# Masked attention with residual: the row step and the norm of a pair each one step later in the hand-written order

## The chip, the cores and the metric

The kernel runs on one core of one Trainium2 chip. The metric is the device time of one execution in microseconds (us), lower being better. A core has the engines TensorE (PE, matmuls; its weight loads are listed as PEld), VectorE (DVE), ScalarE (ACT), GpSimd (POOL), which here mainly issues gathers and scatters, and SyncE (SP), which here issues all other transfers. SBUF is the on-chip memory, PSUM the small memory that TensorE writes to.

## The reference

Sixteen batches of a tensor `x` (512 channels by 1024 tokens) go through an attention with eight heads of 64 channels. A token whose mask is 0 takes no part as a key, and as a query it gets equal scores, which is the mean over all tokens. The result is added to `x`.

```python
xt = transpose(x)                            # (16, 1024, 512)
q  = xt @ Wq.T                               # queries, keys and values are the same
scores = 0.125 * einsum('bhqd,bhkd->bhqk', qh, qh)
logits = (scores * cmask + (1 - cmask) * -1e30) * rmask
ctx = einsum('bhqk,bhkd->bhqd', softmax(logits), qh)
out = x + transpose(ctx @ Wo.T)
```

About half of the tokens are unmasked. What the kernel does exploits that.

## The kernel before, in words

For each batch `b` the unmasked tokens, at most 544 of them, are gathered into a compact list. Only these go through scores, softmax and the projection; their result is added to their rows of `x` and scattered back. The masked tokens all get the same vector (the projection of the mean), added elsewhere. Products are made from float16 parts, high and low (`xh` and `xl`, `ch` and `cl`, `wqh` and `wql`), so one product is three matmuls.

The eight heads are worked as four pairs `p` = 0 to 3. A batch is a list `S` of 18 steps: four steps (p, i), i = 0 to 3, for each pair, each for 128 of the keys, and two steps (0, None) at place 2 and (1, None) at place 13 for the last 32 keys of four heads together. In the list, pair 0 ends at step 4, pair 1 at step 8, pair 2 at step 12 and pair 3 at step 17.

What a step issues, in this order:
- jobs that were put in the dictionary `free` for this step;
- the scores of the first head of the pair (L620, four matmuls into `pss`, of which there are two buffers; then the exponential on ACT, L624, which also sums the rows into `z`);
- a share of the batch's other work, the list `m`, given out by `fill` in proportion to fixed costs: queries of the next batch (L447 with its ACT copy L450, the split into `hl` L461 to L463 on DVE, and the copies `xx` L468 to L471 on SP), values (L497, L500), value tails (L520, L523), transposes of the gathered rows (L424, with L384 on ACT and L385 on DVE), the mean token's columns (L381, L382), the shift of the softmax (L541, L543, L549, L551, L558, L560 and the lines to L572), and projections of the batch before (L727 on PE, L732 on DVE);
- the scores of the second head, and at i = 1 the attends of the pair before (L643, 16 matmuls into `pav`) at a raised priority;
- at i = 2 the last part of the pair before (L647, four matmuls, which need the copies `pt` that L604 and L605 prepare on DVE and L611 and L612 issue on SP), and the copy of `pav` to `c` on ACT (L651).

A pair's softmax sums become a factor for each query in three jobs:
- `recip_sums` (L666 to L674, DVE): from the sums in `z` and `zt` the reciprocals, a column `rcol` for the pair; two such columns are used in turn.
- `recip_rows`: PE transposes the column (L680) into a `pm` buffer, DVE copies ten rows out (L683, `rr`, raised priority), SP writes them to DRAM (L685, `rd`) and reads them back twice as rows broadcast over 64 partitions each (two issues of L688, `rb`, two buffers).
- `norm` (DVE): L711 multiplies `c` by `rb`, L712 adds the mean's part, L714 and L715 split into `ch` and `cl`, L716 and L717 do the same for the last 32 queries; for pair 0 also L707 and L708. L711 is held behind the latest scores or query matmul at the moment of its issue (`self.beat`), except for pair 3.

For pairs 0 to 2 these jobs are put into `free` when the pair's last step `st` is issued: the sums for `st + 2`, the rows for `st + 3`, the norm for `st + 7`, at most the last step, 17. The norm of pair 2 is put there only in the last batch; in the others it stands in the list `m` of the next batch (named `second` there). Pair 3's three jobs all stand in the next batch's `m` (`sums`, `rows`, `third`).

So in a batch the rows of pairs 0, 1 and 2 are issued at steps 7, 11 and 15, and the norms of pairs 0 and 1 at steps 11 and 15.

Issue order is not yet the order on the engines. A list scheduler with priorities orders the instructions of each engine, the raised ones ahead; buffers are taken from pools (`pm`, `pss` two each, `rb` two, `c` four, `p` twelve), and an engine works its instructions strictly in its order. A waiting instruction holds up all behind it on its engine.

Of the kernel before, what the change touches and what calls it, by code (L numbers as in the profile page):

```python
# [49 lines left out]
class Fast:  # L50
# [794 lines left out]
    def run(self, flag):  # L845
        B = self.B
        L = lambda f, *a: lambda: f(*a)
# [3 lines left out]
        N = len(S)  # L851
# [93 lines left out]
        if True:  # L945
            for b in range(B + 1):
# [4 lines left out]
                free, sums, rows, third, tail, rest = {}, [], [], [], [], []  # L951
# [68 lines left out]
                def fill(part, end=False):  # L1020
                    nonlocal done, goal, pos
                    goal += part * unit
                    while pos < len(m) and (end or (part and done + m[pos][0] / 2 <= goal)):
                        m[pos][1]()
                        done += m[pos][0]
                        pos += 1

                for st, (p, i) in enumerate(S):
                    soon, self.soon = self.soon, []
                    for f in soon + free.get(st, []):  # L1030
                        f()
                    if i is None:
                        self.scores(b, p, None)
                    else:
                        ps = [self.scores(b, 2 * p, i)]
                        if i == 2 and whole:
                            whole.pop()()
                    fill(share[st][0], st == N - 1)
                    if i is not None:
                        ps.append(self.scores(b, 2 * p + 1, i))  # L1040

                    for _ in range(1 if b < B - 2 else -(-len(self.urgent + self.spare) // (N - st))):
                        self.issue()

                    if i == 0:
                        ready, todo = todo, []
                    elif i == 1:
                        self.group_first = None
                        for f in ready[3::-1] + ready[4:]:
                            f()  # L1050
                        ready = []
                    fill(share[st][1])
                    if i is not None:
                        todo.append(L(self.attend, b, p, i, ps))
                    if i == 3:
                        (whole if p < 3 else todo).append(L(self.attend, b, p, 4, None))
                        if p < 3:
                            free.setdefault(st + 2, []).append(L(self.recip_sums, b, p))
                            free.setdefault(st + 3, []).append(L(self.recip_rows, b, p))
                            if p < 2 or b == B - 1:  # L1060
                                free.setdefault(min(st + 7, N - 1), []).append(L(self.norm, b, p))
                self.st.pop(b - 4, None)
        bad = self.const.tile([1, 1], F32, name="bad")
        self.nc.vector.tensor_reduce(bad, self.ok[0:1, :], AX.X, ALU.add)
# [145 lines left out]
```

## Time and profile before

| | |
|---|---|
| three timed runs | 1070.66, 1070.85 and 1076.17 us, median 1070.85 |
| the profiled execution | 1064.91 us, its span 1063.1 us |
| granted TensorE clock in it | 0.992 |
| DMA | 181.37 MB moved, mean 171 GB/s |
| one batch | about 63.3 us |
| L711 on DVE, 64 times | 722 ns each |
| L624 (exponential) on ACT, 512 times | 718 ns each |
| L620 on PE, 2048 matmuls | 307.0 us busy, 6.5 us idle before them |
| L680 on PE, 64 times | PE idle before them: 6.3 us until `rcol` L674 (9 times), 0.7 us until the exponential L624 (once) |

The page was taken from one execution by the hardware profiler. "Busy" is the time that an engine's instructions took; the ends of matmuls are modelled, and they overlap. A line such as `PE pm L680 <- DVE rcol L674` says that PE sat idle ahead of the instruction at line 680 that writes the tile `pm`, until the instruction at line 674, which writes `rcol` on DVE, was done. A timeline row has the start in us, the duration in us, engine, line, operation, out and in tiles with their sizes, how many like it in a row, and in brackets the idle time ahead of it and what ended it.

### The profile page before, as it was taken

How to read it: one execution, taken by the hardware profiler on the slowest of the kernel's cores; microseconds unless marked ns; L12 is line 12 of the kernel's file. 1: busy time of each engine (PE TensorE's matmuls, PEld its weight loads, DVE VectorE, ACT ScalarE, POOL GpSimd, SP SyncE). 2: the span in 40 equal slices, each digit the busy share in tenths (PEclk: the TensorE clock that was granted, in tenths of full speed). 3: DMA queues.
4: the chain of work that ended last, by engine and by line, in shares of the span. 5: the costliest groups of instructions: out<-in, count | busy, mean ns of one | idle time of the engine just before them, and what ended most of it. 6: DMA issues, size and time to landing. Idle time of an engine off the chain costs nothing.

```text
span 1063.1 us, 23765 instructions
## 1 busy us (share of the span) xinstructions
PE 1021.6 (96%) x8626; PEld 701.6 (66%) x8626; DVE 729.2 (69%) x2376; ACT 672.5 (63%) x1722; POOL 298.6 (28%) x303
## 2 busy tenths in 40 slices
PE   7798999999999999999999999999999999999996
PEld 7576666666666767666676666767666676766553
DVE  6697668676766856776775766876676776666653
ACT  5876666666676766666676576676666676664550
POOL 3101013322301222332322223232232332235652
PEclk9899999999999999999999999999999999999998
DMA  6746555546654665766557575655856554575752
GB/s 206 226 132 166 136 166 165 177 142 204 174 145 137 160 189 156 195 194 165 173 149 210 167 199 172 162 166 148 239 174 179 170 159 144 142 195 170 222 172 76
DMA packets 78123, 181.37 MB, mean 171 GB/s; under 512 B 15008, under 2 KB 16800, under 8 KB 78000
## 3 DMA queue, kind: packets, MB, share of 16 engines
q1 hardware_dynamic: 56816, 111.62, 38.4%
q0 software_dynamic: 21184, 68.18, 20.5%
q8 instruction: 70, 1.15, 0.5%
q14 instruction: 53, 0.43, 0.1%
HBM read 92.34 MB, written 33.91 MB: 119 GB/s over the span
## 4 chain that ended last, share of the span: by engine, by line
PE 76%; ACT 10%; DVE 7%; issue 3%; DMA 2%; POOL 0%; POOLq 0%; DVEq 0%; SPq 0%; ACTq 0%
PE pav L643 22%; PE pss L620 17%; PE pm L727 15%; PE pm L447 12%; ACT p L624 5%; PE pm L424 2%; PE pav L647 2%; ACT xh L384 1%; DVE p L605 1%; ACT xm L369 1%; PE pss L595 1%; PE pm L497 1%; PE pm L680 1%; ACT v L500 1%; ACT p L599 1%
## 5 line engine op out<-in xcount | busy, mean ns | idle before, releaser
L624 ACT ACTIVATE p<-pss,nm 128x544 f32<-128x544 f32 x512 | 365.4, 718 | 217.5 <-PE pss L620 203.6
L620 PE MATMUL pss<-xx 128*128 128x272 f16 x2048 | 307.0, 280 | 6.5 <-ACT p L624 5.7
L643 PE MATMUL pav<-p,v 128*64 128x272 f32 x2048 | 248.8, 396 | 0.0
L620 PEld LDWEIGHTS <-xx 128*128 128x128 f16 x2048 | 194.7, 99 | 63.3 <-issue 22.5
L643 PEld LDWEIGHTS pav<-p,v 128*64 128x64 f32 x2048 | 141.4, 137 | 91.0 <-issue 13.9
L811 POOL DMA_INDIRECT y_out<-xa,idx x68 | 72.1, 1060 | 292.8 <-PE pss L620 150.2
L447 PE MATMUL pm<-xh,wqh 128*128 128x274 f16 (+1 forms) x512 | 143.9, 281 | 2.4 <-DVE xa L732 1.9
L447 PE MATMUL pm<-xh,wql 128*128 128x274 f16 (+1 forms) x512 | 143.2, 280 | 0.0
L447 PE MATMUL pm<-xl,wqh 128*128 128x274 f16 (+1 forms) x512 | 143.1, 280 | 0.0
L339 POOL DMA_INDIRECT xa<-x_in,idx x68 | 67.9, 999 | 210.6 <-PE pss L620 101.5
L447 PEld LDWEIGHTS <-wqh 128*128 128x128 f16 x1024 | 98.1, 99 | 25.8 <-issue 4.8
L624 ACT ACTIVATION_READ_ACCUMULATOR p<-pss,nm 128x1 f32 x512 | 104.0, 203 | 0.0
L811 POOL DMA_INDIRECT y_out<-xi,idx x60 | 69.5, 1159 | 107.5 <-PE pss L620 49.0
L727 PE MATMUL pm<-woh,ch 128*128 128x512 f16 x240 | 91.1, 380 | 0.0
L727 PE MATMUL pm<-woh,cl 128*128 128x512 f16 x240 | 90.9, 379 | 0.0
L727 PE MATMUL pm<-wol,ch 128*128 128x512 f16 x240 | 90.9, 379 | 0.0
L450 ACT ACTIVATE q<-pm 128x272 f32<-128x272 f32 (+1 forms) x128 | 50.9, 398 | 63.0 <-PE pm L447 62.8
L339 POOL DMA_INDIRECT xi<-x_in,idx x60 | 61.4, 1023 | 102.2 <-PE pss L620 43.5
L732 DVE SCALAR_TENSOR_TENSOR xa<-pm,xa 128x512 f32<-128x512 f32 x60 | 41.3, 688 | 63.3 <-PE pm L727 59.9
L727 PEld LDWEIGHTS <-ch 128*128 128x128 f16 x480 | 45.6, 98 | 45.9 <-issue 1.4
L798 DVE TENSOR_TENSOR xi<-xi,ub 128x512 f32<-128x512 f32 (+1 forms) x60 | 40.9, 688 | 42.6 <-PE pss L620 42.0
L711 DVE TENSOR_TENSOR c<-c,rb 128x544 f32<-128x544 f32 x64 | 46.2, 722 | 28.0 <-PE pm L447 17.1
(194 smaller groups left out, 1558.4 us busy)
## 6 DMA issues: line engine op xcount, KB each, us to landing
xx<-hl SPq DMA_DIRECT2D x256, 136.0 KB
xm<-x_nat_in SPq DMA_DIRECT2D x56, 512.0 KB
rb<-rd SPq DMA_DIRECT2D x128, 136.0 KB
pt<-c SPq DMA_DIRECT2D x64, 136.0 KB
pt<-p SPq DMA_DIRECT2D x64, 136.0 KB
ub<-ud SPq DMA_DIRECT2D x16, 256.0 KB
xi<-x_nat_in SPq DMA_DIRECT2D x8, 256.0 KB
xa<-x_in,idx POOLq DMA_INDIRECT x68, 4.6
```

What stands on the lines that cost most here:

```text
L339: dma = self.nc.gpsimd.indirect_dma_start(out=tile[:n], out_offset=None, in_=self.x, in_offset=bass.IndirectOffsetOnAxis(ap=idx, axis=0))
L424: self.pe = nc.tensor.transpose(pt[:, c, :], x[:n, c * P:(c + 1) * P], self.ident[:n, :n]).ins
L447: self.beat = nc.tensor.matmul(pq, lhsT=w[:, c, e * P:(e + 1) * P], rhs=xx[:, c, cols], start=(k == 0), stop=(k == 3 * DC - 1)).ins
L450: nc.scalar.activation(s["q"][:, e, cols], pq, AF.Copy, scale=1.0 / (SX * SW))
L620: self.beat = nc.tensor.matmul(pt[:, g, :CH], lhsT=xx[:, 2 * k, i * P:(i + 1) * P], rhs=xx[:, 2 * k + a, g * CH:(g + 1) * CH], start=(a == ...
L624: self.exp = [nc.scalar.activation(t.rearrange("p (g c) -> p g c", g=2), pt[:, :, :CH], AF.Exp, bias=s["nm"][p // HG][:, p % HG:p % HG + 1 ...
L643: mm = nc.tensor.matmul(s["pav"][k * DK:(k + 1) * DK, g, :CH], lhsT=s["v"][p][:, i, k * DK:(k + 1) * DK], rhs=ps[k][:, cols], start=(i == ...
L711: self.once(nc.vector.tensor_tensor(c, c, s["rb"][p], ALU.mult), self.beat if p < 3 else None)
L727: nc.tensor.matmul(po[:cols.stop - cols.start], lhsT=a[:, e, cols], rhs=w[:, e, :], start=(e == 0 and k == 0), stop=(e == DC - 1 and k == 2))
L732: self.nc.vector.scalar_tensor_tensor(x, po, 1.0 / (SX * SW), x, ALU.mult, ALU.add)
L798: self.once(self.nc.vector.tensor_tensor(x[:n], x[:n], s["ub"][:n], ALU.add), self.beat)
L811: dma = self.nc.gpsimd.indirect_dma_start(out=self.out, out_offset=bass.IndirectOffsetOnAxis(ap=idx, axis=0), in_=x, in_offset=None)
```

## The change

Two numbers in `run` change. The rows of pairs 0, 1 and 2 are put into `free` for four steps after the pair's end, not three: steps 8, 12 and 16. The norms of pairs 0 and 1 are put there for eight steps after it, not seven: steps 12 and 16. In the last batch the norm of pair 2 stays at step 17, the last one, while its rows move. The sums (`recip_sums`) stay where they are, as do pair 2's norm in the other batches and all of pair 3. No instruction is added or removed on any engine; their order changes.

```diff
                         if p < 3:
                             free.setdefault(st + 2, []).append(L(self.recip_sums, b, p))
-                            free.setdefault(st + 3, []).append(L(self.recip_rows, b, p))
+                            free.setdefault(st + 4, []).append(L(self.recip_rows, b, p))
                             if p < 2 or b == B - 1:
-                                free.setdefault(min(st + 7, N - 1), []).append(L(self.norm, b, p))
+                                free.setdefault(min(st + 8, N - 1), []).append(L(self.norm, b, p))
```

## The prediction

> **What bounds the kernel now.** I read the share of busy time first, then the chain that ended last, then what TensorE (PE) waited for. The first line below is busy time per engine, the second the chain's share per engine.
>
> ```profile
> PE 1021.6 (96%) x8626; PEld 701.6 (66%) x8626; DVE 729.2 (69%) x2376; ACT 672.5 (63%) x1722; POOL 298.6 (28%) x303
> PE 76%; ACT 10%; DVE 7%; issue 3%; DMA 2%; POOL 0%; POOLq 0%; DVEq 0%; SPq 0%; ACTq 0%
> ```
>
> PE is the bound nearly everywhere, and the change adds no instruction to any engine, so only PE's idle gaps can move. Going through PE's records one by one I count 73 gaps of together 29 us, about 12 of them in the first 100 us. That is what there is to win or to double. The view of waits names those gaps (wait: us in total, times, longest):
>
> ```profile
> PE pm L680 <- DVE rcol L674: 6.3, 9, 0.7
> PE pss L620 <- ACT p L624: 5.7, 13, 0.7
> PE pm L447 <- DVE xa L732: 1.9, 5, 0.4
> PE pm L680 <- ACT p L624: 0.7, 1, 0.7
> ```
>
> The dearest repeated gap is the very instruction that is moved, the transpose L680 of `recip_rows`: ten times, always pair 2 (batches 1, 3, 4, 6, 7, 9, 10, 12, 13, 14), 0.70 us each (batch 14: 0.63). Batch 6 shows how (PE, DVE and SP rows in order of time):
>
> ```profile
> 463.98 0.28 PE L558 MATMUL pm<-ident,m 128*128 128x4 f32 x2
> 464.65 0.17 DVE L674 TENSOR_TENSOR rcol<-rcol,hit 128x10 f32<-128x10 f32 x1
> 464.76 0.73 DVE L711 TENSOR_TENSOR c<-c,rb 128x544 f32<-128x544 f32 x1
> 464.97 0.30 PE L680 MATMUL pm<-ident,rcol 128*128 128x128 f32 x1 [0.70 <-DVE rcol L674]
> 467.64 0.19 DVE L717 TENSOR_TENSOR ctl<-c,cth 128x32 f16<-128x32 f32 x1
> 471.56 0.17 DVE L381 CAST xh<-ms 128x4 f16<-128x4 f32 x1 [3.72 <-PE pm L447]
> 476.28 0.69 DVE L732 SCALAR_TENSOR_TENSOR xa<-pm,xa 128x512 f32<-128x512 f32 x1 [1.02 <-PE pm L727]
> 476.89 0.41 DVE L523 TENSOR_TENSOR tmp<-pm,par 128x256 f32<-128x256 f32 x1
> 477.23 1.04 PE L424 MATMUL pm<-ident,xa 128*128 128x128 f32 x8
> ```
>
> PE reaches L680 before DVE has made `rcol`; then pair 1's norm (L711 to L717) follows, and DVE idles 3.72 us before L381. From L381 to L732 it works with 1.02 us of idle time, and L424, which needs the buffer that L732 empties, starts 0.26 us after L732's end. Those two lines are the cover that the change uses up.
>
> **The change part by part.** The two programs' instruction orders, set side by side without running, show where the steps go. Each L680 keeps its 0.11 us of PE (start to the next start).
>
> *Pair 2's rows, step 15 to 16.* L680 now stands behind a dozen of L447 (1.4 us) and more, so `rcol` is ready: −0.70 in each of batches 1, 3, 4, 6, 7, 9, 10, 12, 13.
>
> *Pair 1's norm, step 15 to 16.* In those nine batches L711 to L717 and L683 now stand between L381 and L732. I add start-to-start times: L711 0.64, L712 0.30, L714 0.33, L715 0.60, L716 and L717 0.20, L683 0.20, less L708 (0.17, now behind L523). Interleaved with L382 to L485 they close some 0.4 us of small waits for results that the old order has, so DVE reaches L732 5.35 us after L381 instead of 4.72, while PE's product is there at 4.83 (one L680 more in between). L732 is 0.52 late, L424 has 0.26 of cover, so a new stall of about 0.3. Without the closing it is 0.8; if DVE packs tighter, 0. I take 0.3, because the old rows already start 0.07 to 0.08 us before the one ahead ends where nothing depends.
>
> Batches 3, 6, 7, 9, 10, 12, 13: −0.70 + 0.30, seven times: **−2.8**. In batches 1 and 4 the bottom's first matmul L549 also comes after only half a group of scores and waits for L543, which stands behind pair 0's norm and an L732: about 0.5 more, bounds 0 and 1.0. Two times +0.1: **+0.2**.
>
> *Batches 2, 5, 8, 11.* Here L447's wait for L732 (0.37 to 0.45) goes: −1.6. The norm of pair 0 and an L732 now stand ahead of L604 and L605, so the two `pt` copies are issued 1.7 us later and land 0.7 to 1.0 later; the attend L647 that needs them also comes 0.86 earlier on PE in some of these batches. Their landings have a margin of 0.45 us in batch 2, 1.60 in 5, 1.83 in 8 and 0.63 in 11. So two batches pay 0.2 to 0.4: **−1.0** (bounds −3.5 with the earlier L647 kept as gain, +2.5 with a late copy in all four).
>
> *Batch 14* has both stalls (0.45 and 0.63) and the last batches' dense gathers: **−0.5**, bounds −1.1 and +0.5. *Batch 0*: three groups of scores now follow each other without other work between, and PE stalls of L620 for the exponential are 0.4 to 0.7 long: **+0.75**, bounds 0 and 1.5.
>
> *Pair 0's rows, step 7 to 8.* In seven batches L680 now stands five score groups' matmuls ahead of L520, and that needs the buffer that L683 empties: about 0.1 each, **+0.7**, bounds 0 and 2. Pair 1's rows meet no wait either way. In the last batch pair 2's rows move and its norm stays at step 17; there L711 already waits 1.53 us for `rb`, but the projections that need it have about 1.4 us of margin: 0, bounds 0 and +2.
>
> *SP's queue and pair 2's norm in the next batch.* This norm does not move, its data do. Of each moved step the DMAs L685 (`rd`) and two L688 (`rb`) move too. Before:
>
> ```profile
> DVE c L711 <- DMA rb<-rd: 4.4, 5, 1.5
> SPq L688 <- DMA rd<-rr: 83.5, 45, 4.6
> 471.25 1.11 SPq L688 DMA_DIRECT2D rb<-rd  x2
> 473.61 0.48 SPq L468 DMA_DIRECT2D xx<-hl  x1
> ```
>
> L685 now passes the 512 KB load L374 and the `pt` copies (its landing was 5.05 us behind them, 1.2 alone), but L468 now stands between `rd` and `rb` and waits for L463, which comes 2.2 us later behind pair 1's norm. By batch 6's clock: rows at 472.7, L468 at 475.8, L688 at 476.3 and 476.85. An `rb` lands 2.3 to 4.8 us after its issue in the DMA records, so at 479.2 to 481.6. DVE comes to L711 at about 478.7, and behind L711 stand both L385, which free the buffers for the next L424 at about 482.9. L711 and the two L385 take 1.95, so DVE may wait 2.2 to 2.6 us before PE notices. The wait is 0.5 to 2.9; I take its middle, which is hidden: **0**, bounds 0 and +0.7 for each of 13 batches.
>
> [...]
>
> **The sum.** −2.8 + 0.2 − 1.0 − 0.5 + 0.75 + 0.7 + 0 = −2.65 us. The profiled execution took 1064.91 (span 1063.1): it becomes 1062.3. The three timed runs have their median at 1070.85, 0.55% above that execution, so I put the same difference on the median: **1068.2**. A measurement of this kernel can tell about 0.5% (5.35 us) from no change, and this forecast lies inside: no difference that counts, with a lean to faster.
>
> **Rivals.**
> *Full gain.* If DVE packs tighter than I add, no new stall follows at L424, L549 and L647: ten stalls (6.9) and five (2.1) go, and batch 0 and pair 0's rows give back 1.45: −7.6, so 1063.3. For it speaks DVE's 69% and the 3.72 us hole just ahead; against it, that the hole lies before L381 and the norm now behind it. Chance 0.31, with the cases between this and the forecast beyond −5.35.
> *DVE blocked by a late `rb`.* Place: L711 of pair 2's norm at the head of DVE's queue in the next batch, with both L385 behind it. Price: 0.5 to 1.0 us of PE in 13 batches, +6.5 to +13 on the sum, so 1074.7 to 1081.2. It decides at a landing later than about 4.5 us after the issue of L688 (a DVE wait over 2.4 us), since the nearest rows end at 4.8 and L374 and four `xx` copies of 136 KB are issued around it. Against it: most landings lie under 3.5. With the case that the norm behind L381 costs its full 0.8 us in nine batches (+4.5 on the sum) and more at L549: chance 0.27.
> *The change does nothing.* The wait is only handed from L680 to L424 one for one, and the rest cancels: 1070 to 1072. This belongs to the forecast's side of the bounds.
>
> **Chances and range.** Within 0.5%: 0.42 (forecast, and the change that does nothing). Faster 0.31. Slower 0.27. Likeliest case alone: 1065.5 to 1073. The range that should hold 8 in 10 goes from the full gain with batches 2 to 11 at their good end (1061.5) into the blocked DVE at a little under half its price (1077.0).
>
> **What would show it.** Right: the wait of L680 for L674 vanishes from PE's list; a new wait of L424 for L732 of about 0.3 us appears some nine times; L447's wait for L732 shrinks; DVE's idle time before L381 grows to about 6 us and that before L732 vanishes; DVE's wait of L711 for `rb` grows from 4.4 to 10 us or more, while L424's wait for L385 stays away. Wrong: L424 waits for L385 over ten times (the blocked DVE), L647 waits for `pt` in most batches, or L680 still waits. If PE's gaps sum to within 3 us of 29 and the time still moves by over 0.5%, the whole way of counting gaps is wrong.

## The result, and the profile after

The changed kernel is slower: 1087.42 us (median of 4, 1085.91 to 1091.26) against 1071.03 us of the kernel before in the same runs. The ratio is 1.0154, with a 95% interval of 1.0135 to 1.0173. The forecast was 1068.2, its range ended at 1077.0. The profiled execution after took 1088.17 us, its span is 1086.5 us. The two spans differ by 23.4 us, more than the medians, because the first trace of the kernel before lies 6 us below its timed runs.

The two lines of the page that answer to those shown before (busy time, and the chain that ended last):

```profile
PE 1031.7 (95%) x8626; PEld 702.4 (65%) x8626; DVE 720.3 (66%) x2376; ACT 672.0 (62%) x1722; POOL 366.2 (34%) x303
PE 73%; ACT 7%; DMA 7%; DVE 6%; issue 4%; POOL 1%; SPq 1%; POOLq 0%; another core or an unknown queue 0%; DVEq 0%; ACTq 0%
```

The same number of matmuls has 10 us more of busy time, and DMA has gone from 2% of the chain to 7%. The view of PE's waits (us in total, times, longest) says where:

```profile
PE pav L647 <- DMA pt<-p: 10.9, 5, 3.2
PE pss L620 <- ACT p L624: 9.4, 13, 2.9
PE pm L424 <- DVE xa L732: 0.4, 1, 0.4
```

L680 is gone from the list, as forecast, and so is L447's wait for L732. In their place stands L647, the last part of pair 2's attend, waiting for the copies `pt`. Counted over all PE records, the idle gaps rise from 29.4 to 42.7 us.

To see which batches pay, I cut each batch in two at its two groups of tail scores (L595, at steps 2 and 13) and compare the pieces with the kernel before. A second trace of that kernel (e0, below) repeats 27 of the 29 pieces from batch 1 on within 0.02 us (the other two differ by 0.18 and 1.31), so differences of 0.1 us count. The four columns are the pieces from step 13 of batches 2, 5, 8 and 11 to step 2 of the next (26.5 us each before); the last is the mean of the same piece of batches 3, 6, 7, 9, 10, 12 and 13. All in us against the kernel before; the experiments are described below.

| kernel | 2 | 5 | 8 | 11 | mean of seven |
|---|---|---|---|---|---|
| changed | +3.53 | +4.18 | +2.05 | +4.57 | −0.24 |
| e3, pair 0 alone | +1.13 | +1.30 | +0.98 | +3.49 | −0.53 |
| e4, pair 1 alone | +1.20 | −0.51 | −0.51 | +0.78 | +0.32 |
| e5, pair 2's rows alone | +0.03 | +0.03 | +0.04 | +0.03 | −0.65 |
| e8, pairs 0 and 1 | +2.48 | +3.92 | +3.49 | +4.21 | −0.44 |
| e9, pairs 1 and 2 | +0.34 | −0.56 | −0.57 | −0.57 | −0.49 |
| e6, changed, no wait for `pt` | −0.52 | −0.51 | −0.51 | −0.52 | −0.09 |
| e7, changed, warm matmuls | +1.79 | +1.76 | +1.65 | +1.82 | −0.40 |
| e12, changed, norm 0 back in four | +1.26 | −0.58 | −0.57 | −0.37 | +0.07 |
| e14, changed, load later in four | +2.57 | +0.57 | +1.15 | +3.90 | −0.19 |

Four batches lose 14.3 us together; nearly all of the rest lies at the two ends of the run (see "The ends" below). Batch 5 of the changed kernel shows how the loss is made. First DVE and SP of the changed kernel in order of time:

```profile
400.20 0.69 DVE L798 TENSOR_TENSOR xi<-xi,ub 128x512 f32<-128x512 f32 x1 [5.05 <-PE pss L620]
403.17 0.70 DVE L711 TENSOR_TENSOR c<-c,rb 128x544 f32<-128x544 f32 x1
405.71 0.67 DVE L715 TENSOR_TENSOR cl<-c,ch 128x512 f16<-128x512 f32 x1
407.20 0.48 SPq L468 DMA_DIRECT2D xx<-hl  x1
407.65 0.28 DVE L463 COPY hl<-hl 128x544 f16<-128x544 f16 x1
407.94 0.42 DVE L604 CAST c<-p 128x544 fp32r<-128x544 f32 x1
408.44 0.71 DVE L605 TENSOR_TENSOR p<-p,c 128x544 fp32r<-128x544 f32 x1
409.13 1.04 SPq L471 DMA_DIRECT2D xx<-hl  x1
410.27 0.55 SPq L611 DMA_DIRECT2D pt<-c  x1
411.16 0.81 SPq L612 DMA_DIRECT2D pt<-p  x1
```

The same steps in the kernel before (the whole is 7.7 us earlier there; its L595 group starts at 395.46, the other at 403.15):

```profile
387.49 0.72 DVE L711 TENSOR_TENSOR c<-c,rb 128x544 f32<-128x544 f32 x1
392.69 0.69 DVE L798 TENSOR_TENSOR xi<-xi,ub 128x512 f32<-128x512 f32 x1 [2.36 <-PE pss L620]
397.85 0.29 DVE L463 COPY hl<-hl 128x544 f16<-128x544 f16 x1
398.14 0.44 DVE L604 CAST c<-p 128x544 fp32r<-128x544 f32 x1
400.50 0.54 SPq L611 DMA_DIRECT2D pt<-c  x1
401.15 0.76 SPq L612 DMA_DIRECT2D pt<-p  x1
```

Before, pair 0's norm ran at 387.49, ahead of a hole of 2.36 us in DVE's work. Now it stands at 403.17, behind that hole, which has grown to 5.05 us, and inside the split of the third query block. Counted from the start of the L595 group, L604 starts at 4.79 us instead of 2.68, and the first `pt<-p` is issued at 8.02 instead of 5.69, behind four `xx` copies which wait for the same split. It lands at 13.6 instead of 10.1 (landings from the DMA's semaphore records). PE wants L647 at 10.95, before at 11.71. So it waits, and then something else happens (PE's rows):

```profile
416.89 0.62 PE L647 MATMUL pav<-pt,vt 128*128 128x272 f32 x3 [2.79 <-DMA pt<-p]
417.95 0.29 PE L447 MATMUL pm<-xh,wqh 128*128 128x274 f16 x1
418.08 0.28 PE L447 MATMUL pm<-xl,wqh 128*128 128x274 f16 x1
419.02 0.43 PE L447 MATMUL pm<-xh,wqh 128*128 128x274 f16 x1
419.24 0.43 PE L447 MATMUL pm<-xl,wqh 128*128 128x274 f16 x1
```

The window of that stretch (us, then busy time and instructions of PE, PEld, DVE, ACT and POOL, granted clock, DMA share, GB/s):

```profile
418.00:421.00 3.00, 3.00 (x16) 2.07 (x16) 0.60 (x6) 1.79 (x5) 0.00 (x0) 0.55 0.26 95
```

The matmuls behind the wait first follow each other in 0.12 us, then in 0.23, and the granted clock is 0.55. What this slow stretch costs can be read against e6 (below), the changed kernel without the wait for `pt`: in these four pieces PE works the same matmuls in the same order in both, and the changed kernel takes 4.05, 4.69, 2.57 and 5.09 us longer. Its waits for `pt` are 2.16, 2.79, 2.33 and 3.16 us. So 1.89, 1.90, 0.24 and 1.93 us are left, and the profile grants half clock for 3.41 us behind the first, second and fourth wait and not behind the third, so about 0.2 us in each has another cause. At half clock such a stretch can cost up to 1.7 us (an estimate: half of the 3.41 us at a granted clock of 0.50). Against the kernel before, the four pieces lose less, 14.33 instead of 16.40 us together, because e6 itself is 0.5 us below it in each.

### The profile page after: what moved, and what is told of

Its sections match the earlier page's. It is cut to its first block, busy times and chain, and to the rows that moved or that the text cites. A ratio compares the mean times of both kernels' runs of the same rounds, so it can differ in the third digit from the quotient of the medians.

```text
span 1086.5 us, 23761 instructions
## 1 busy us (share of the span) xinstructions
PE 1031.7 (95%) x8626; PEld 702.4 (65%) x8626; DVE 720.3 (66%) x2376; ACT 672.0 (62%) x1722; POOL 366.2 (34%) x303
## 3 DMA queue, kind: packets, MB, share of 16 engines
q8 instruction: 70, 1.15, 0.5%
## 4 chain that ended last, share of the span: by engine, by line
PE 73%; ACT 7%; DMA 7%; DVE 6%; issue 4%; POOL 1%; SPq 1%; POOLq 0%; another core or an unknown queue 0%; DVEq 0%; ACTq 0%
PE pav L643 19%; PE pss L620 17%; PE pm L727 14%; PE pm L447 13%; ACT p L624 4%; PE pm L424 2%; PE pav L647 2%; DMA pt<-p 2%; DMA rb<-rd 1%; DMA xa<-x_in,idx 1%; POOL xa L339 1%; PE pss L595 1%; DMA xx<-hl 1%; ACT xh L384 1%; PE pm L497 1%
## 5 line engine op out<-in xcount | busy, mean ns | idle before, releaser
L620 PE MATMUL pss<-xx 128*128 128x272 f16 x2048 | 309.9, 280 | 11.7 <-ACT p L624 9.4
L620 PEld LDWEIGHTS <-xx 128*128 128x128 f16 x2048 | 194.4, 99 | 71.4 <-issue 29.6
L811 POOL DMA_INDIRECT y_out<-xa,idx x68 | 76.2, 1121 | 277.3 <-PE pss L620 186.5
L339 POOL DMA_INDIRECT xa<-x_in,idx x68 | 89.9, 1323 | 189.7 <-PE pss L620 57.0
L447 PE MATMUL pm<-xh,wqh 128*128 128x274 f16 (+1 forms) x512 | 145.4, 284 | 0.7 <-DVE nm L560 0.4
L447 PE MATMUL pm<-xl,wqh 128*128 128x274 f16 (+1 forms) x512 | 144.8, 283 | 0.2 <-DVE xl L385 0.2
L447 PE MATMUL pm<-xh,wql 128*128 128x274 f16 (+1 forms) x512 | 144.7, 283 | 0.0
L811 POOL DMA_INDIRECT y_out<-xi,idx x60 | 110.1, 1834 | 97.4 <-PE pss L620 39.0
L447 PEld LDWEIGHTS <-wqh 128*128 128x128 f16 x1024 | 99.8, 100 | 22.8 <-issue 2.6
L732 DVE SCALAR_TENSOR_TENSOR xa<-pm,xa 128x512 f32<-128x512 f32 x60 | 41.0, 683 | 69.8 <-PE pm L727 66.9
L369 ACT ACTIVATE xm<-xm 128x1024 f32<-128x1024 f32 (+1 forms) x62 | 62.7, 1011 | 1.6 <-DMA xm<-x_nat_in 1.6
```

Source lines behind the costliest of these rows:

```text
L339: dma = self.nc.gpsimd.indirect_dma_start(out=tile[:n], out_offset=None, in_=self.x, in_offset=bass.IndirectOffsetOnAxis(ap=idx, axis=0))
L369: self.nc.scalar.activation(s["xm"][k], s["xm"][k], AF.Copy, accum_out=s["ms2"][:, k:k + 1])
L447: self.beat = nc.tensor.matmul(pq, lhsT=w[:, c, e * P:(e + 1) * P], rhs=xx[:, c, cols], start=(k == 0), stop=(k == 3 * DC - 1)).ins
L620: self.beat = nc.tensor.matmul(pt[:, g, :CH], lhsT=xx[:, 2 * k, i * P:(i + 1) * P], rhs=xx[:, 2 * k + a, g * CH:(g + 1) * CH], start=(a == ...
L732: self.nc.vector.scalar_tensor_tensor(x, po, 1.0 / (SX * SW), x, ALU.mult, ALU.add)
L811: dma = self.nc.gpsimd.indirect_dma_start(out=self.out, out_offset=bass.IndirectOffsetOnAxis(ap=idx, axis=0), in_=x, in_offset=None)
```

## The experiments

The kernel before had medians of 1072.34, 1062.67 and 1071.77 us in the three groups of runs, 0.9% apart. Only ratios within a group are compared.

**One pair at a time: e3, e4, e5.**

```diff
# e3: pair 0 alone          e4: pair 1 alone           e5: pair 2's rows alone
-st + 3  (rows)     -st + 7  (norm)
+st + (4, 3, 3)[p]  +st + (8, 7, 7)[p]     # e3
+st + (3, 4, 3)[p]  +st + (7, 8, 7)[p]     # e4
+st + (3, 3, 4)[p]  +st + (7, 7, 8)[p]     # e5
```

> Only pair 0's rows and norm are a step later; pairs 1 and 2 as before. Theory A (pair 0's norm now stands among the split of the third query block and ahead of L604 and L605, so the copies pt land too late in batches 2, 5, 8 and 11, and PE runs at half clock after each long wait): most of the loss is here, L647 waits 2 us or more for pt in these four batches, the time is 8 to 18 us above the kernel before. Theory B (pair 2's late rb blocks DVE in the next batch): pair 2's rows are untouched, so no change beyond 2 us. Theory C (only the norm of pair 1 behind L381 costs): no change beyond 2 us.

Measured: 1.0035 (1.0011 to 1.0059), 3.8 us above the kernel before, less than theory A's 8 to 18. The waits for `pt` are there (1.48, 1.60, 1.30 and 2.18 us), but only the last is followed by slow matmuls: that piece loses 1.3 us more than its wait, the other three 0.3 us less than theirs. The mechanism is that of A, its size is not.

> Only pair 1's rows and norm are a step later. Theory A: pair 0's norm is out of the way of L604 and L605, but in batches 2, 5, 8 and 11 the attend L643 still moves ahead of a dozen of L447, so L647 comes up to 1.4 us earlier: waits of at most 1 us there, and L424 waits for L732 by 0.3 us in nine batches; 0 to 6 us above the kernel before. Theory C: the norm behind L381 is the cost, 10 us or more above it, with L424's wait for L732 near 1 us nine times. Theory B: no change beyond 2 us.

Measured: 1.0057 (1.0038 to 1.0077), 6.1 us above it, at A's upper edge. Waits of 1.60 us in batch 2 and 1.17 in batch 11, no half clock, and on average 0.32 us more in each of the seven batches. Theory C's 10 us are out.

> Only pair 2's rows are a step later, and its norm in the last batch stays where it is. Theory A: this alone removes the nine or ten waits of L680 (6.3 to 7.0 us) and touches neither pt nor the split: 4 to 7 us below the kernel before. Theory B: rb lands too late for pair 2's norm in the next batch, DVE stands, L424 waits for L385: 3 us or more above the kernel before.

Measured: 0.9939 (0.9915 to 0.9963), 6.5 us below, as A said. L680's waits for `rcol` are gone and no L647 wait has come. Theory B is out.

The three together (3.8 + 6.1 − 6.5 = 3.4) fall 13 us short of the whole change. So parts of it work on each other.

**The wait for `pt` taken away: e6.** L647 reads a constant tile, so the last 32 keys of each head are left out of the sum over values.

```diff
+self.zero32 = fixed("zero32", [P, CH], F32R); nc.gpsimd.memset(self.zero32.bitcast(F32), 0.0)
-rhs=s["pt"][:, p % 2, cols], start=False, stop=(k == 1))
+rhs=self.zero32, start=False, stop=(k == 1))
```

> The changed kernel, but L647 multiplies with a constant tile of zeros instead of pt (the last 32 keys of each head are left out of the sum over values); the copies pt are still issued and all else is the same. Theory A: the four waits of L647 (10.5 us) and the half clock behind them (about 4 us) go: 12 to 16 us below the changed kernel, so 0 to 5 us above the kernel before. Theories B and C: the waits move to another place, less than 5 us below the changed kernel, 11 us or more above the kernel before.

Measured: 0.9996 (0.9978 to 1.0015) of the kernel before. By the two ratios that is 1.6% or 17 us below the changed kernel, a little over A's span. All four columns of the table turn to −0.5. The waits are not handed to another place: this one dependency, with what it sets off, is as large as the whole net loss.

**The kernel before once more: e0.** Nothing is edited.

> The kernel before once more, for a second trace of it: its first profiled execution took 1064.91 us while its timed runs lie at 1070 to 1072. Theory A (the 2 us before the first batch's tail scores and a stop of all engines of 2 to 3 us in the last batch, which every other trace shows, are chance and not of the change): about 1070 us, PE waits of 1 to 2 us more in the first 40 us and one of 1 us or more after 1000 us, while the batches between repeat within 0.2 us each. Theory D (the end is slower because pair 2's rows are later there): the last batch repeats the first trace, no wait over 0.5 us in it.

Measured: 1062.42 us. The stretches repeat, the first batch differs by 4 us in its favour, and the last batch again has no stop (no wait over 0.4 us in it). The time and the first batch are not as theory A says; the last batch is as theory D says. But the next runs speak against D: e7, e8 and e9 of the same group also have no stop in the last batch (0.5 us less than the kernel before), although pair 2's rows are moved in two of them. In the other two groups every kernel with a trace loses 1.6 to 4.7 us there, with or without pair 2's rows (e3 4.5, e4 2.2). The stop goes with the group of runs, each of which ran on a chip of its own, and not with the change. Theory D is out; what the stop is, stays open.

**Warm matmuls in the wait: e7.**

```diff
+self.zero16 = fixed("zero16", [P, P], F16); nc.gpsimd.memset(self.zero16, 0.0)
 def attend(self, b, p, i, ps):
+    for _ in range(12 if i == 4 and p == 2 and b % 3 == 2 and b < 12 else 0):
+        nc.tensor.matmul(s["pav"][:, 0, :CH], lhsT=self.zero16, rhs=self.xh[:, 0, :CH], start=False, stop=False)
```

> The changed kernel, with twelve matmuls by a zero weight into the same sum ahead of L647 of pair 2 in batches 2, 5, 8 and 11 (nothing else is changed; the order on the other engines is the same). They take 1.4 us of the wait for pt, and the four score matmuls behind three of them also move into it. Theory A (PE's half clock follows from the long idle time): the matmuls behind L647 keep their full pace (0.116 us from L447 to L447 instead of 0.227), 4 to 8 us below the changed kernel. Rival (they are slow for another reason, such as the copies' traffic into the memory that PE reads): L447 stays at 0.227 us behind the wait; only the moved scores are gained, at most 2 us below the changed kernel.

Measured: 1.0097 (1.0074 to 1.0120), so by the ratios 0.57% or 6.1 us below the changed kernel. Batch 5 of it on PE (the zero matmuls are L631; nine of the twelve are in the first row):

```profile
410.32 1.21 PE L631 MATMUL pav<-xh,zero 128*128 128x272 f16 x9
412.19 0.74 PE L647 MATMUL pav<-pt,vt 128*128 128x272 f32 x4 [0.67 <-DMA pt<-p]
412.77 0.29 PE L447 MATMUL pm<-xh,wqh 128*128 128x274 f16 x1
412.90 0.28 PE L447 MATMUL pm<-xl,wqh 128*128 128x274 f16 x1
```

Its window, in the same columns:

```profile
411.00:422.00 11.00, 10.33 (x85) 7.31 (x84) 8.73 (x29) 7.03 (x20) 2.77 (x3) 1.00 0.55 161
```

The wait has been filled, and the granted clock of the eleven us behind it is 1.00. All four batches now lose the same 1.7 to 1.8 us. The slow matmuls follow from PE's idle time, not from traffic: in the 7.8 us from L647's start the DMA engines' busy share is 0.52 here and 0.30 in the changed kernel.

**Two pairs at a time: e8 and e9** (edits as above, with (4, 4, 3) and (8, 8, 7), and with (3, 4, 4) and (7, 8, 8)).

> Pairs 0 and 1 a step later, pair 2's rows as before. Theory A with interaction (pair 0's norm ahead of L604 and L605 delays pt, and pair 1's later rows put the attend and L647 earlier and the split of the queries in one block before pt on SP): the four waits for pt are as long as with the whole change, 2 us and more with half clock behind, and no gain from pair 2: 12 to 18 us above the kernel before. Rival (the parts add up): 3.9 and 6.1 us give 8 to 11 us above it.

Measured: 1.0127 (1.0095 to 1.0159), 13.5 us above; the four waits are 2.83, 2.59, 2.32 and 2.87 us, slow stretches follow three of them. The parts do not add: e3 and e4 have 6.9 and 1.0 us in the four columns, together 14.1. Pair 0's norm makes `pt` late, and with pair 1's step it lands about 1 us later still (13.1 to 13.7 us after the L595 group against 11.8 to 13.0 in e3); that carries the waits from about 1.5 us, where no slow stretch followed, to 2.3 and more, where it mostly did.

> Pairs 1 and 2 a step later, pair 0 as before. Theory A: without pair 0's norm in front of L604 and L605 the copies pt come in time or with waits under 1.5 us, no half clock; in the nine other batches the wait of L680 goes (0.87 us with its slot) and L424's for L732 comes (0.4): 4 us below to 3 us above the kernel before. Rival (the loss is made by pairs 1 and 2 together): 8 us or more above it.

Measured: 0.9986 (0.9974 to 0.9997). This is as theory A says. Without pair 0 batch 2 loses 0.34 us and the other three gain 0.6 each; the rival is out.

**Pair 0's norm alone put back: e12.**

```diff
-free.setdefault(min(st + 8, N - 1), []).append(L(self.norm, b, p))
+free.setdefault(min(st + (7 if p == 0 and b % 3 == 2 and b < 12 else 8), N - 1), []).append(L(self.norm, b, p))
```

> The changed kernel, but in batches 2, 5, 8 and 11 alone the norm of pair 0 is back at step 11 (its rows stay at step 8). Theory A (this norm, in front of the split of the queries and of L604 and L605, makes pt late): the four waits for pt and the half clock go, each of these batches is 4 us shorter or more and a little below the kernel before (0.5 us, as without pair 0 at all); the time is 13 to 19 us below the changed kernel, 3 us below to 3 us above the kernel before. Rival (the moved rows of pair 0 and their DMAs are as guilty): half of the loss or more stays, 7 us or more above the kernel before. The norm's move back also lets the scheduler put a load L374 behind pt; the next run tells the two apart.

Measured: 1.0012 (0.9995 to 1.0029): by the ratios 1.42% or 15 us of the loss gone by one number in four batches. In its batch 5 (DVE and SP) the split and L604 come nearly as early as in the kernel before (L604 at 2.85 us after the L595 group at 402.39, before at 2.68), and the load has moved behind the copies:

```profile
404.92 0.29 DVE L463 COPY hl<-hl 128x544 f16<-128x544 f16 x1
405.24 0.45 DVE L604 CAST c<-p 128x544 fp32r<-128x544 f32 x1
408.22 0.55 SPq L612 DMA_DIRECT2D pt<-p  x1
410.56 0.58 SPq L374 DMA_DIRECT2D xm<-x_nat_in  x1
```

In batches 5, 8 and 11 L647 no longer waits; in batch 2 a wait of 1.59 us stays. The moved rows of pair 0 are not the cause.

**The load alone put behind `pt`: e14.**

```diff
-at = 3 * c + (0 if b else 4)
+at = 3 * c + (4 if c == 3 and b % 3 == 2 and b < 12 else 0 if b else 4)
```

> The changed kernel, but the fourth load of 512 KB (L374) for the next batch but one is issued four steps later in batches 2, 5, 8 and 11, so that it stands behind pt in SP's queue; DVE and PE keep their order. Theory A1 (pt is late because DVE makes it late: L605 ends 1.7 us later and the four xx copies, held by L463, stand ahead of it): the waits shrink by less than 0.7 us each, less than 6 us below the changed kernel. Theory A2 (pt is late mainly because the load's bytes and its place fill the queue): pt lands 1.5 us earlier or more, the half clock goes, 8 to 14 us below the changed kernel.

Measured: 1.0092 (1.0067 to 1.0118), by the ratios 6.6 us below the changed kernel, between the two theories. `pt<-p` lands 2.0 and 1.4 us earlier in batches 5 and 8, 0.6 later in batch 2 and 0.7 earlier in batch 11, while its issue moves by −1.2 to +1.1 us. So the load's place matters. But it is not what the change moved: counted from the L595 group, it is issued at 2.15 to 2.36 us in the changed kernel and at 1.98 in the kernel before, ahead of `pt` in both. And e3 has the load at 1.98 like the kernel before, and only pair 0's later norm ahead of the split: its first `pt<-p` lands 0.7, 2.4, 2.0 and 2.0 us later than in the kernel before. DVE's order alone makes `pt` late; the load ahead adds to it. How much belongs to each in batches 2 and 11 is not settled.

**A version that beats both: e13, with e5 again.**

```diff
-st + 3 (rows)                                                     -st + 7 (norm)
+st + (3, 4 if b % 3 == 2 and b < 12 else 3, 4)[p]                 +st + (7, 8 if b % 3 == 2 and b < 12 else 7, 7)[p]
```

> The kernel before with pair 2's rows a step later in all batches, and pair 1's rows and norm a step later in batches 2, 5, 8 and 11 alone; pair 0 as before. Theory A, from the traces so far: pair 2's rows bring 0.87 us in each of nine batches, pair 1's step brings 0.56 in each of the four: 7 to 11 us below the kernel before. Rival (gains of one batch come back as waits in the next): less than 4 us below.

> Pair 2's rows alone once more, on the same chip as the version above, to compare the two. Theory A: 6 to 8 us below the kernel before, and 1 to 3 us above the version that also moves pair 1 in four batches. Rival: the first result was due to a stop at the end of the batches that had nothing to do with it, within 3 us of the kernel before.

Measured: e13 0.9939 (0.9921 to 0.9957), e5 again 0.9945 (0.9920 to 0.9970). Both beat the kernel before by about 6 us, e13 with less than the 7 to 11 expected. Pair 1's extra step gains 0.57 us in three of its four batches and loses 0.95 in batch 2, so the two versions can't be told apart. The simpler one, pair 2's rows alone, is the one to keep.

## Why the prediction was wrong

*Pair 2's rows:* right. The waits of L680 went: −0.70 was forecast, and in e5, where they move alone, the same pieces of the nine batches give −0.70 on average, −0.87 to −0.89 in five of them.

*Pair 1's norm behind L381:* right to a tenth. Batch 6 of the changed kernel on DVE and PE:

```profile
482.30 0.18 DVE L381 CAST xh<-ms 128x4 f16<-128x4 f32 x1 [1.29 <-PE pm L447]
482.38 0.72 DVE L711 TENSOR_TENSOR c<-c,rb 128x544 f32<-128x544 f32 x1
487.53 0.68 DVE L732 SCALAR_TENSOR_TENSOR xa<-pm,xa 128x512 f32<-128x512 f32 x1
488.27 1.09 PE L424 MATMUL pm<-ident,xa 128*128 128x128 f32 x8
490.11 0.74 DVE L711 TENSOR_TENSOR c<-c,rb 128x544 f32<-128x544 f32 x1 [0.54 <-DMA rb<-rd]
```

L732 starts 5.23 us after L381 (forecast 5.35), with no idle time ahead of it, and PE's stretch from the first L520 before L424 to the L620 behind it is 2.27 us instead of 2.02 (486.94 to 489.20; before 476.08 to 478.10). The forecast gave this stall 0.3. As a wait it hardly shows in the list (once, 0.4), since the modelled ends of the matmuls ahead of it cover a step of 0.25 us. The stretches between starts show it. The seven batches brought −0.24 each on average where −0.40 was forecast (−1.7 instead of −2.8 us), batches 1 and 4 −0.07 and +0.06 where +0.1 was. One sign failed: DVE's idle time before L381 did not grow from 3.72 to about 6 us, it is 1.29 in batch 6, because the lines L560 to L572 now lie in that hole. Batch 14 lost 0.62 us where −0.5 was forecast, just over the bound of +0.5; no run was made to find why.

*DVE blocked by a late `rb` (the slower rival):* it did not happen. DVE's wait of L711 for `rb` grew from 4.4 to 10.6 us, as forecast for the harmless case, 0.54 of it in the last line above, and L424 does not wait for L385. The chance of a slower result was put on the wrong mechanism.

*Batches 2, 5, 8 and 11:* this is the step that failed, "land 0.7 to 1.0 later" and "two batches pay 0.2 to 0.4: −1.0". It had the place, the copies, their margins and the cause, and it failed three times in the size. First, the later landing: the first `pt<-p` was issued 2.0 to 3.0 us later, not 1.7, and landed 1.7, 3.5, 3.3 and 3.0 us later. The time from issue to landing shrank in batch 2 alone (5.5 to 4.3 us); in the others it grew, from 4.2 to 5.4 before to 4.5 to 6.4. Second, L647's being earlier on PE was sized well (0.86 against 0.76), but the price of 0.2 to 0.4 is the later landing less the margin alone, in batches 2 and 11. Where the 0.86 has to be taken off the margin too, the forecast's own numbers give waits of 1.1 to 1.4 us in batch 2 and 0.9 to 1.2 in batch 11. Margins of 0.45 to 1.83 us less 0.76 could not hold what was measured: waits of 10.4 us in place of 0.6. Third, a wait was priced one for one: the half clock behind three of them added about 5 us. The term was −1.0 with bounds of −3.5 and +2.5; it is +14.3.

*The landings.* The forecast read 2.3 to 4.8 us from the issue of `rb` to its landing. In the kernel before they took 2.8 to 5.7 us and in the changed kernel 2.7 to 5.4 (there the 55 copies of 128 whose landing records are complete), and the first `pt<-p` in the four batches of the changed kernel 4.3 to 6.4.

*Pair 0's rows* were put at +0.7. The pieces from step 2 to step 13 of batches 1 to 14 together are 1.4 us longer than before, 0.8 of it in batch 2. That 0.8 also stands in every other kernel of the groups with the stop (e5 too, where pair 0 is not moved), and not in e0. So about 0.6 is left, near the forecast.

*The ends.* Batch 0 with the start (forecast +0.75) and the last batch (0) lie 3.3 and 3.5 us above the kernel before in the traces, and what follows the last L595 group 1.9. Runs of other kernels scatter by as much there, so these amounts belong to no step. In the last batch three engines stand together: ACT, DVE and PE sit idle for 1.53, 2.14 and 2.89 us before 1017.96, 1018.02 and 1018.82.

## What to carry to other kernels

When a step of an engine off the critical path is moved later, ask which hole of that engine it leaves and what stands behind it in the new place, and follow each of these to its transfer and to the consumer's margin; the consumer may come earlier at the same time, so both eat the same margin. Move dependent steps one by one: here one of three moves brought the gain, and the other two together, harmless in most of the batches, took it back twice over in the four where the margins were short. Price a long wait of the matmul engine above its own length: three of the four waits for `pt` here, of 2.16, 2.79 and 3.16 us, had 3.41 us at a granted clock of 0.50 behind them, worth up to 1.7 us more by the estimate above.

## What the runs showed of the hardware

After 50 us the half-clock stretches in the changed kernel's trace are 3.41 us long, but for the last one, which begins at 1080.48 and runs to the end. From 50 us on PE has eight waits of more than 1.1 us (us from the start of the span):

| PE idle | its length | ahead of | granted clock behind it |
|---|---|---|---|
| 84.09 to 86.01 | 1.91 | L497 | 1.00 |
| 97.49 to 99.12 | 1.63 | L497 | 1.00 |
| 220.98 to 223.13 | 2.16 | L647, batch 2 | 0.50 from 223.73 to 227.14 |
| 414.10 to 416.89 | 2.79 | L647, batch 5 | 0.50 from 418.29 to 421.70 |
| 607.65 to 609.98 | 2.33 | L647, batch 8 | 1.00 |
| 799.67 to 802.83 | 3.16 | L647, batch 11 | 0.50 from 804.00 to 807.41 |
| 1015.93 to 1018.82 | 2.89 | L620 | 0.50 from 1019.04 to 1022.45 |
| 1052.42 to 1054.20 | 1.78 | L620 | 1.00 |

The kernel before has one such wait after 50 us, of 2.39 us (86.20 to 88.60, ahead of L647), and the granted clock behind it is 1.00.

The waits for `pt` of 1.17 to 1.60 us in e3, e4 and e12 had no half clock behind them either: each of their pieces loses 0.3 to 0.4 us less than its wait. Length alone does not decide among the longer ones: 2.33 and 2.39 us went without, and so did 2.83 in batch 2 of e8 (its piece loses 2.48), while 2.16 went with, and 2.18 in batch 11 of e3 (its piece loses 3.49). What decides was not shown: in these runs the place and the length of the waits changed together. The ends of matmuls are modelled, so these idle times are no more exact than the model.
